# A plan with other durations, and the first half of the first group ahead of everything: a four-stage transformer block on one core

## The chip, the core and the metric

The kernel runs on one core of one Trainium2 chip. The metric is the device time of one execution in microseconds (us). A core has five engines that work side by side, each through its own list of instructions in order: TensorE (PE, matrix products), VectorE (DVE), ScalarE (ACT), GpSimd (POOL) and SyncE (SP, which here issues every DMA). An instruction that waits for another engine holds up everything behind it on its own engine.

## The reference

`x` is 8 sequences of 1024 rows of 256 numbers, all in fp32. Four stages follow each other; each is added to its own input:

```python
x = x + attn_0(layernorm(x))   # linear "flow" attention, 16 heads of 16, then a GELU feed-forward of 1024
x = x + ffn_0(layernorm(x))    # ReLU feed-forward, 256 -> 1024 -> 256
x = x + attn_1(layernorm(x))   # one head of softmax attention, 256 wide, over 1024 rows
x = x + ffn_1(layernorm(x))    # weights and activations rounded to blocks of FP4, SiLU gate, 256 -> 704 -> 256
```

The change touches mostly the first stage. Its core, for each head (`cumsum` runs over the rows of a sequence):

```python
q, k = sigmoid(q), sigmoid(k)
sink_in  = normal / sum_d((q + EPS) * (cumsum(k) + EPS))      # normal = 1, 2, 3, ...
src_out  = normal / sum_d((k + EPS) * (cumsum(q) + EPS))
cons_sink = sum_d((q + EPS) * (cumsum(k * src_out) + EPS)) / normal
cons_src  = sum_d((k + EPS) * (cumsum(q * sink_in) + EPS)) / normal
sink_alloc = sigmoid(cons_sink)
src = exp(clip(cons_src, -1, 1))
v = v * src / cumsum(src) * normal
x = ((q * sink_in / normal) @ cumsum(k^T v)) * sink_alloc
```

`cumsum(k^T v)` makes this causal: within a chunk of 128 rows the kernel forms the scores `k q`, keeps those with key not after query, and multiplies by `v`; what earlier chunks contribute comes from a running sum of `k^T v` (the tile `kv_sum`). The scores are sums of products of sigmoids, so they are positive.

## The kernel before, in words

Rows are worked on in **chunks** of 128 and **groups** of four chunks (512 rows); there are 16 groups, two to a sequence. For the first stage:

- `front` normalises a chunk (`n`) and transposes it into `n0T`; it also adds a bias to the chunk on GpSimd (`res`).
- `linear_span` takes a group, or in group 0 a half group of two chunks ("near"): projections to `q` and `k` (sigmoid on ACT), running sums (`running`, a scan on DVE with a carried column, `carry_cur` or `carry_w`), products with the other of `q` and `k` (`prod`), sums over the 16 numbers of a head as PE products with `hsum`, a reciprocal, and the weights `flow`, which are spread again over the rows of a head: by DMA through DRAM (`packed`, `spread`) for a whole group, by a PE product with a mask (`spread_near`) for a half group. Then the same again with weighted tiles, and from those sums `e`, `div` and `scale`.
- `linear_chunk` scales `v`, makes the zero-padded queries `qz`, four banks of scores, masks them (`sc`, by a product with `triu` on DVE), multiplies with `v` (`sc,v_pad`), adds the running `kv_sum`, projects with `wo`, adds `res`, normalises (`h`), and transposes into a `half` of two chunks.

`dense` runs both feed-forward layers by half groups: for each of eight slices of 128 hidden columns, two products `half,w_ff`, an activation on ACT (`hidden`), and two products `w_ff,hidden` a few slices later. `norms_1` and `norms_2` are the layer norms after them. `soft_chunk` does the third and fourth stage of one chunk, once its whole sequence has been normalised.

**What sets the order.** All this is written as Python generators, "parts", that yield what the next step needs: an engine (`pe`, `dve`, `act`, `dma`), tiles, free PSUM banks, a buffer, a due time `at`. `Plan.run` picks, at each step, the part that has to wait least for PE, then the one whose operands have been ready for long enough (`RIPE`), then the one with the earliest due time. `Plan.took` gives each recorded instruction a duration by a formula for its engine, and keeps when each engine and each tile is free. All five engines are pinned to this order of issue (`add_manual_dep` in `Queue`), so it is the plan's durations, not the chip's, that decide the order in which each engine works. A wrong duration makes no wrong result; it makes an engine wait in front of an instruction whose operands aren't there yet. The due times are in units of groups: `p + 0.1`, `p + 0.15` and so on for group `p`; the second half group of group 0 is due 0.25 later (`after`).

Every instruction is issued by one helper, so all have the same line, L315, in the profile; the tiles' names tell them apart. On PE there are two "tiled" forms (`prod,hsum`, `sc,v_pad`, `q,kv_sum`, `v_pad,k` on 32 columns and `qz,k` on 32 rows), of which four run side by side. An fp32 product is recorded as two passes, a transpose as one.

Of the kernel before, what the change touches and what calls it, by code (L numbers as in the profile page):

```python
# [16 lines left out]
P = 128  # L17
# [12 lines left out]
G = 4  # L30
# [32 lines left out]
class Plan:  # L63
# [12 lines left out]
    def __init__(self, tc, nc):  # L76
# [14 lines left out]
        self.act_set = 0  # L91
        self.tiled = False
# [65 lines left out]
    def took(self, queue, op, args, kw):  # L158
# [11 lines left out]
        after = 0.06  # L170
        if queue == "tensor":
# [3 lines left out]
            cost = size * (0.84e-3 if op == "transpose" else 1.68e-3)  # L175
            tiled = op == "matmul" and (kw["lhsT"].shape[-1] <= 32 or kw["lhsT"].shape[0] <= 32)
            if tiled:
                cost *= 0.25
# [4 lines left out]
        elif queue == "vector":  # L183
            each = {"reciprocal": 6.2e-3, "tensor_tensor_scan": 2.15e-3}.get(op, 1.05e-3)
            cost = 0.15 + each * size
            if op == "tensor_scalar" and outs[0].dtype == BF16:
                cost = 0.16 + 0.26e-3 * size
        elif queue == "scalar":
            cost = (0.16 if op == "copy" else 0.26) + 0.82e-3 * size
            for x in args:  # L190
                if not isinstance(x, bass.AP) and self.SETS.get(x, self.act_set) != self.act_set:
                    self.act_set = self.SETS[x]
                    cost += 1.3
# [8 lines left out]
        start = self.free.get(queue, 0.0)  # L202
        for ap in aps:
            name = ap.tensor.name
            if self.by.get(name) != queue:
                start = max(start, self.done.get(name, 0.0))
            if name not in self.done and name in self.held:
                start = max(start, self.used[name])
        if queue == "tensor":
# [4 lines left out]
            self.ran = start + cost  # L214
        end = start + cost
# [6 lines left out]
        self.free[queue] = end  # L222
# [30 lines left out]

    def ready(self, need):
# [19 lines left out]
    def run(self):  # L274
        while self.parts:
            now = self.free.get("tensor", 0.0)
            best = None
            for part in self.parts:
# [5 lines left out]
                wait = max(max(t) - now - (0.3 if stays else 0.0), 0.0)  # L284
                unripe = max(t[1] + self.RIPE[queue] - now, 0.0)
# [48 lines left out]
def block_stack_kernel(ctx: ExitStack, tc: tile.TileContext, a: dict, out: bass.AP):  # L334
# [115 lines left out]
    pos = const.tile([P, P], F32, name="pos")  # L450
    nc.vector.tensor_copy(pos, pos_i)
# [20 lines left out]
    mask_tiles = [make("prob", "mask") for _ in range(2)]  # L472
    late = set()

    def masks():
        yield act(ident, at=0.02)
        for b in range(4):
# [12 lines left out]
    def late_constants():  # L490
# [10 lines left out]
        late.add("hsum")  # L501
        yield dve()
# [3 lines left out]
        for g in range(NG):  # L506
            yield dve()
            nc.vector.tensor_scalar(rpos[:, g, :], pos, float(g * GT), None, ALU.add)
            yield dve()
            nc.vector.reciprocal(rpos[:, g, :], rpos[:, g, :])  # L510
# [71 lines left out]
    def layernorm_affine(dst, src, gain, shift):  # L582

        mean, rstd = ln_stats(src)
# [7 lines left out]
    def turned(srcs):  # L592
# [4 lines left out]
        return bank[:, : len(srcs), :]  # L597

# [213 lines left out]
    def running(out, cur, carry, b, first, last):  # L812
# [9 lines left out]
        if not last:  # L822
            nc.vector.tensor_copy(carry[:, b : b + 1], out[:, cur.shape[1] - 1 :])
# [45 lines left out]
    def linear_group(p):  # L869
# [34 lines left out]
        for i in range(G):  # L904
            plan.start(front(i), p + 0.03 * i)
# [19 lines left out]
    def linear_span(p, span, fronts, tiles):  # L925
# [13 lines left out]
        after = 0.25 if span.start else 0.0  # L939
        near = len(span) < G  # L940

# [32 lines left out]
        for n, b in enumerate((2, 0, 3, 1)):  # L974
            other = (b + 2) % 4
            prods[other] = yield from fresh(
                "flow", dve(cur[b], at=p + 0.15 + 0.04 * n + after, when=turn("flow")), "prod"
            )
            prod = prods[other][:, :width]
            running(prod, cur[b], past["cur"], b, opens, closes)  # L980
            yield dve(cur[other])
            nc.vector.scalar_tensor_tensor(prod, cur[other], ATT_EPS, prod, ALU.add, ALU.mult)
# [6 lines left out]
        nc.vector.scalar_tensor_tensor(flow, pos[rows], float(g * GT), r1, ALU.add, ALU.mult)  # L989
# [7 lines left out]
        for n, b in enumerate((2, 0, 3, 1)):  # L997
            other = (b + 2) % 4
            w = weighted[b]
            need = dve(w, at=p + 0.35 + 0.04 * n + after, when=turn("scale"))  # L1000
            if near:
                weighted[b] = yield from fresh("flow", need, "weighted")
            else:
                yield need
            out = weighted[b][:, :width]
            nc.vector.tensor_tensor(out, cur[b], w[:, :width], ALU.mult)
            if near and n % 2:
                plan.let_go(w)
            prods[other] = yield from fresh("flow", dve(), "prod")
            prod = prods[other][:, :width]  # L1010
            running(prod, out, past["w"], b, opens, closes)
            plan.drop(weighted[b])
            yield dve()
            nc.vector.scalar_tensor_tensor(prod, cur[other], ATT_EPS, prod, ALU.add, ALU.mult)
# [34 lines left out]
        nc.vector.scalar_tensor_tensor(e, pos[rows], float(g * GT), e, ALU.add, ALU.mult)  # L1049
        nc.vector.tensor_scalar(e, e, src[rows], None, ALU.mult)  # L1050
# [34 lines left out]
    def linear_chunk(p, i, n0T, comp, qk):  # L1085

        s, g = divmod(p, NG)
        past, c = seqs[s]["past"], p * G + i
        here = slice(i * P, (i + 1) * P)
# [6 lines left out]
        for k in range(2):  # L1096
# [25 lines left out]
                at=p + 0.62 + 0.06 * i,  # L1122
# [7 lines left out]
        qz = tile_qz.rearrange("p (k e t) -> p k e t", k=2, e=2)  # L1130
        for e in range(2):
# [4 lines left out]
        yield pe(qz, banks=4, tiled=True)  # L1136
        banks = []
        for r in range(4):
            rows = slice(32 * r, 32 * r + 32)
            bank = mm_bank()  # L1140
            banks.append(bank)
            for k in range(2):
# [4 lines left out]
                    start=True,  # L1147
                    stop=True,
                )
        plan.drop(tile_qz)  # L1150
        scores = []
        for bank in banks:
            sc = yield from fresh("flow", dve(bank), "sc")
            sc = sc.rearrange("p (n t) -> p n t", n=4)
# [473 lines left out]
```

## Time and profile before

| | us |
|---|---|
| median of three runs | 2684.94 (2684.01 to 2687.68) |
| the profiled execution, its own time | 2683.53 |
| span of its instructions | 2681.8 |
| granted PE clock, mean | 0.991 of full |
| PE idle before `hsum` products, waiting for `prod`, whole span | 12.3, in 11 waits |
| PE idle waiting for `n` | 11.2, in 7 waits |
| PE idle waiting for ACT `prob` | 7.7, in 9 waits |
| ACT table loads | 320 of 1283 ns |
| DVE masking of scores, 128x512 | 256 of 681 ns |

In a row of the profile, `bank<-half,w_ff` is a product that reads `half` and `w_ff` and writes a PSUM bank, `x4` are four records in a row, and `[4.28 <-DVE prod]` says that the engine stood idle for 4.28 us before it and that the instruction of DVE that writes `prod` ended the wait. PEclk is the clock that the chip granted PE.

### The profile page before, as it was taken

The page shows a single profiled execution, that of the slowest core. Times are in us where ns is not written, and L with a number is a line of the kernel's source. Part 1 is how long each engine was busy: PE and PEld are TensorE (multiplying, and loading weights), DVE is VectorE, ACT ScalarE, POOL GpSimd, SP SyncE. Part 2 cuts the span into 40 slices and gives each one's busy share as a digit, 9 for nine tenths or more (in the row PEclk, how much of TensorE's full clock was granted, in tenths as well). Part 3 has the DMA queues.
Part 4 walks back from the last instruction along what each step waited for, and adds up shares of the span by engine and source line. Part 5 has one row for each costly group of instructions (what it writes and reads, how often), then busy time and mean ns, then how long its engine had stood idle before and what let it go on. Part 6 is the DMA issues. An engine that isn't in the chain of part 4 may idle for free.

```text
span 2681.8 us, 45726 instructions
## 1 busy us (share of the span) xinstructions
PE 2600.9 (97%) x16687; PEld 2016.8 (75%) x16687; DVE 1971.2 (74%) x4514; ACT 1258.6 (47%) x2442; POOL 585.4 (22%) x1101
## 2 busy tenths in 40 slices
PE   6999999999999999999999999999999999999998
PEld 4777777787777777777777777777777777787765
DVE  8779787867768768586786858778586876856576
ACT  2443544445444453545536464363544546344343
POOL 1332322222212313123131212213122131212000
PEclk8999999999999999999999999999999999999999
DMA  3334231323223222232323223132231322322100
GB/s 87 101 106 144 85 101 58 107 66 87 73 64 107 75 77 72 77 101 62 97 66 94 81 72 107 52 90 79 68 108 58 97 64 73 91 66 82 41 12 12
DMA packets 286815, 211.89 MB, mean 79 GB/s; under 512 B 24704, under 2 KB 275072, under 8 KB 286592
## 3 DMA queue, kind: packets, MB, share of 16 engines
q1 hardware_dynamic: 286592, 208.97, 26.7%
q8 instruction: 133, 2.18, 0.3%
q14 instruction: 90, 0.74, 0.1%
HBM read 188.17 MB, written 20.71 MB: 78 GB/s over the span
## 4 chain that ended last, share of the span: by engine, by line
PE 72%; DVE 18%; DMA 4%; ACT 2%; issue 1%; POOL 1%; SPq 0%; DVEq 0%; ACTq 0%; POOLq 0%
PE bank L315 72%; DVE prod L315 3%; DVE hid L315 2%; DMA spread<-packed 2%; DVE n L315 2%; DVE ln_st L315 1%; DVE div L315 1%; DVE u L315 1%; DVE spread L315 1%; DVE x_amax L315 1%; DVE res L315 1%; ACT L315 1%; DVE e L315 1%; DVE mx L315 1%; DVE q L315 1%
## 5 line engine op out<-in xcount | busy, mean ns | idle before, releaser
L315 PE MATMUL bank<-half,w_ff 128*128 128x256 f32 x2048 | 532.5, 383 | 8.3 <-DMA w_ff<-in_L_ffn_w_dram 3.8
L315 PE MATMUL bank<-w_ff,hidden 128*128 128x256 f32 x2048 | 530.5, 383 | 0.0
L315 ACT ACT_TABLE_LOAD x320 | 410.6, 1283 | 81.2 <-PE bank L315 76.6
L315 PEld LDWEIGHTS bank<-half,w_ff 128*128 128x128 f32 x2048 | 380.2, 191 | 81.7 <-issue 23.9
L315 PEld LDWEIGHTS bank<-w_ff,hidden 128*128 128x128 f32 x2048 | 370.1, 191 | 83.9 <-issue 39.3
L315 POOL TENSOR_SCALAR ln_ve<-ln_mv 128x1 f32<-128x1 f32 x384 | 95.5, 249 | 1434.3 <-DVE ln_mv L315 1424.2
L315 ACT ACTIVATE hidden<-bank,c_L_ffn_b 128x256 f32<-128x256 f32 x256 | 121.0, 473 | 319.0 <-PE bank L315 318.8
L315 POOL TENSOR_TENSOR ln_rstd<-ln_ve,neghalf 128x1 f32<-128x1 f32 x384 | 240.8, 627 | 32.0
L315 PE MATMUL bank<-n2T,qT 128*128 128x512 f32 x512 | 241.6, 595 | 0.9 <-ACT qT L315 0.9
L315 PE MATMUL bank<-vt,probT 128*128 128x256 f32 x1024 | 233.5, 382 | 0.0
L315 PEld LDWEIGHTS bank<-vt,probT 128*128 128x128 f32 x1024 | 194.3, 191 | 29.9 <-issue 2.3
L315 ACT ACTIVATE hidden<-bank,c_L_attn_b 128x256 f32<-128x256 f32 x256 | 121.6, 475 | 171.0 <-PE bank L315 169.5
L315 PE MATMUL bank<-wdT,hqT 128*128 128x256 f32 x768 | 178.4, 383 | 1.9 <-ACT hqT L315 1.9
L315 PE MATMUL bank<-wgT,xqT 128*128 128x352 f32 x512 | 173.6, 462 | 1.1 <-ACT xqT L315 0.9
L315 PE MATMUL bank<-wuT,xqT 128*128 128x352 f32 x512 | 172.4, 459 | 0.0
L315 DVE TENSOR_TENSOR sc<-bank,triu 128x512 f32<-128x512 f32 x256 | 159.8, 681 | 13.8 <-PE bank L315 13.4
L315 PEld LDWEIGHTS bank<-wdT,hqT 128*128 128x128 f32 x768 | 145.4, 192 | 22.5 <-ACT hqT L315 2.8
L315 DVE TENSOR_TENSOR hid<-hid,bank 128x352 f32<-128x352 f32 x118 | 60.9, 516 | 131.5 <-PE bank L315 88.2
L315 PEld LDWEIGHTS bank<-n2T,qT 128*128 128x128 f32 x512 | 93.1, 190 | 72.1 <-issue 63.3
L315 PEld LDWEIGHTS bank<-wuT,xqT 128*128 128x128 f32 x512 | 97.4, 190 | 54.1
L315 PEld LDWEIGHTS bank<-wgT,xqT 128*128 128x128 f32 x512 | 93.4, 190 | 39.5 <-issue 6.0
L315 DVE TENSOR_REDUCE mx<-bank 128x1 f32<-128x512 f32 x128 | 86.7, 677 | 45.7 <-PE bank L315 45.2
(214 smaller groups left out, 4365.0 us busy)
## 6 DMA issues: line engine op xcount, KB each, us to landing
w_ff<-in_L_attn_W_dram SPq DMA_DIRECT2D x512, 128.0 KB
w_ff<-in_L_ffn_w_dram SPq DMA_DIRECT2D x512, 128.0 KB
spread<-packed SPq DMA_DIRECT2D x90, 256.0 KB
x<-in_L_attn_inputs_dram SPq DMA_DIRECT2D x64, 128.0 KB
xr<-in_L_attn_inputs_dram SPq DMA_DIRECT2D x64, 128.0 KB
rows<-res SPq DMA_DIRECT2D x64, 128.0 KB
out_dram<-y SPq DMA_DIRECT2D x64, 128.0 KB
rows<-rows SPq DMA_DIRECT2D x56, 128.0 KB
```

The costliest lines, as they stand in the source:

```text
L315: ins = method(*args, **kw)
```

## The change

It has these parts; the order of the instructions changes on every engine from the first ten microseconds to the end.

- `Plan.took`: other durations. A result is ready for other engines 0.035 instead of 0.06 after its end; DVE and ACT instructions overlap by 0.08 and 0.1; PE columns cost 0.853e-3 and 1.687e-3 instead of 0.84e-3 and 1.68e-3; bf16 products cost a quarter; a table load is charged to the engine and not to the result; reading an accumulator costs 0.15; outputs wait for their last readers; DVE and GpSimd wait also for their own results; a DMA waits for the eighth DMA before it to land.
- GpSimd steps get a `yield` of their own (`plan.pool`), so that the plan places them when their operands are there; in `norms_1` the addition to `xr`, which waits for a DMA, now stands behind the statistics.
- The carried columns are copied by ACT instead of DVE, with a `yield`; the flows go in pairs (scan, scan, product, product). A product overwrites the tile that the copy reads.
- `kv` of both halves is multiplied by `bdiag` in one DVE instruction; `pos` has a slice for each of the two groups of a sequence; `e` takes one instruction fewer.
- `table`: ahead of `hidden`, where the function set changes, a one-column activation that needs no product, so that the table load stands ahead of the wait for the bank.
- Group 0's first two chunks are due one unit earlier (`at`, negative), and a part with negative due time is taken 0.3 earlier and needs not be ripe; the second half group's `after` of 0.25 stays.
- In group 0 (`by_act`) the mask is a bf16 product: `later` holds an identity and, for each position that has to go, -2^100; it is multiplied into the bank first, the scores are added, and ACT takes the Relu into `sc`. For the other groups DVE masks as before.

```diff
@@ Plan.took
-        after = 0.06
+        overlap, after = 0.0, 0.035
         if queue == "tensor":
...
-            if tiled:
+            if tiled or op == "matmul" and kw["lhsT"].dtype == BF16:
                 cost *= 0.25
...
+            overlap = 0.08
         elif queue == "scalar":
...
-                    cost += 1.3
+                    self.free[queue] = self.free.get(queue, 0.0) + 1.3
+            if kw.get("accum_out") is not None:
+                cost += 0.15
+            overlap = 0.1
...
+        if queue not in ("tensor", "sync"):
+            start = max([start] + [self.used.get(ap.tensor.name, 0.0) for ap in outs])
         for ap in aps:
             name = ap.tensor.name
-            if self.by.get(name) != queue:
-                start = max(start, self.done.get(name, 0.0))
+            if self.by.get(name) != queue or queue in ("vector", "gpsimd"):
+                start = max(start, self.done.get(name, 0.0) + (0.05 if queue == "gpsimd" else 0.0))
...
+        if queue == "sync":
+            start = max(start, self.landed.pop(0))
...
-        self.free[queue] = end
+        self.free[queue] = end - overlap
@@ Plan.run
-                wait = max(max(t) - now - (0.3 if stays else 0.0), 0.0)
-                unripe = max(t[1] + self.RIPE[queue] - now, 0.0)
+                wait = max(max(t) - now - (0.3 if stays or part[2] < 0.0 else 0.0), 0.0)
+                urgent = part[2] < 0.0
+                unripe = 0.0 if urgent else max(t[1] + self.RIPE[queue] - now, 0.0)
@@ late_constants
+        yield dve(triu)
+        nc.vector.tensor_scalar(
+            later[:, :GT].rearrange("p (n t) -> p n t", n=4),
+            triu.unsqueeze(1).to_broadcast([P, 4, P]),
+            -1.0,
+            2.0**100,
+            ALU.add,
+            ALU.mult,
+        )
@@ table, new
+    def table(func):
+        if plan.act_set != plan.SETS.get(func, plan.act_set):
+            nc.scalar.activation(small([P, 1], "table", 1), one, func)
@@ running
-            nc.vector.tensor_copy(carry[:, b : b + 1], out[:, cur.shape[1] - 1 :])
+            yield act(out)
+            nc.scalar.copy(carry[:, b : b + 1], out[:, cur.shape[1] - 1 :])
@@ linear_group
-            plan.start(front(i), p + 0.03 * i)
+            plan.start(front(i), p + 0.03 * i - (p == 0 and i < 2))
@@ linear_span
-        after = 0.25 if span.start else 0.0
+        after = 0.25 if span.start else -1.0 if near else 0.0
...
-        for n, b in enumerate((2, 0, 3, 1)):
...
+        for n, pair in enumerate(((2, 0), (3, 1))):
+            for b in pair:
+                need = dve(cur[b], at=p + 0.15 + 0.08 * n + after, when=turn("flow"))
+                prod = prods[(b + 2) % 4] = (yield from fresh("flow", need, "prod"))[:, :width]
+                yield from running(prod, cur[b], past["cur"], b, opens, closes)
+            for b in pair:
+                yield dve(cur[b], prods[b])
+                nc.vector.scalar_tensor_tensor(
+                    prods[b], cur[b], ATT_EPS, prods[b], ALU.add, ALU.mult
+                )
@@ linear_chunk
+        by_act = p == 0
...
+        banks = [mm_bank() for _ in range(4)]
+        for bank in banks:
+            if by_act:
+                nc.tensor.matmul(
+                    bank, lhsT=later[:, GT:], rhs=later[:, :GT], start=True, stop=False,
+                    skip_group_check=True,
+                )
...
-            sc = yield from fresh("flow", dve(bank), "sc")
+            sc = yield from fresh("flow", (act if by_act else dve)(bank), "sc")
             sc = sc.rearrange("p (n t) -> p n t", n=4)
+            if by_act:
+                nc.scalar.activation(sc, bank.rearrange("p (n t) -> p n t", n=4), AF.Relu)
+                scores.append(sc)
+                continue
...
+            yield plan.pool(new)
...
+        yield plan.pool(h)
         nc.gpsimd.tensor_tensor(rc, h, b2, ALU.add)
@@ norms_1
-        nc.gpsimd.tensor_tensor(xr, xr, ln2b, ALU.add)
...
-        yield from layernorm_affine(xc, u, ln2g, xr)
+        stats = ln_stats(u)
+        yield plan.pool(xr)
+        nc.gpsimd.tensor_tensor(xr, xr, ln2b, ALU.add)
+        yield from layernorm_affine(xc, u, ln2g, xr, stats)
```

## The prediction

> **What bounds the kernel now.** I read four views in this order: the page, the windows by stage, the waits of the matmul engine (PE) by stage, and the timeline of the first 75 us. The page first:
>
> ```profile
> span 2681.8 us, 45726 instructions
> PE 2600.9 (97%) x16687; PEld 2016.8 (75%) x16687; DVE 1971.2 (74%) x4514; ACT 1258.6 (47%) x2442; POOL 585.4 (22%) x1101
> PE   6999999999999999999999999999999999999998
> PEclk8999999999999999999999999999999999999999
> ```
>
> PE bounds it; DVE, the next engine, has a quarter of the span free. A plan that only orders the same work can win no more than the time in which PE stands still or runs slowly. The windows show where that is:
>
> ```profile
> 0.00:91.00 91.00, 67.51 (x557) 50.31 (x558) 73.22 (x194) 28.28 (x68) 23.26 (x56) 0.81 0.30 78
> 91.00:300.00 209.00, 194.46 (x1513) 156.26 (x1512) 174.56 (x435) 85.63 (x208) 61.60 (x119) 0.98 0.42 122
> 300.00:2500.00 2200.00, 2173.88 (x13910) 1690.77 (x13909) 1602.61 (x3611) 1073.94 (x2027) 492.35 (x905) 1.00 0.27 80
> 2500.00:2682.00 182.00, 165.05 (x713) 119.46 (x711) 120.79 (x276) 70.80 (x140) 8.23 (x22) 0.98 0.05 15
> ```
>
> The columns are stretch, length, busy time of PE, weight load, DVE, ACT and POOL, then clock and DMA. PE idles 91 - 67.5 = 23.5 us of the first 91 and has 0.81 of its clock there, which is 0.19 x 91 = 17 us more; it idles 14.5 us from 91 to 300, 26 in the 2200 us after that, 17 in the tail. So some 98 us are to be had at all, 40 of them in the first 3% of the span. Who is waited for in those first 91 us:
>
> ```profile
> PE bank L315 <- DVE prod L315: 8.5, 7, 4.3
> PE bank L315 <- DVE n L315: 7.8, 2, 7.4
> PE bank L315 <- DVE scale L315: 2.6, 1, 2.6
> ```
>
> And from 300 to 2500 (us in total, times, longest):
>
> ```profile
> PE bank L315 <- DVE v L315: 6.5, 9, 1.1
> PE bank L315 <- ACT prob L315: 5.4, 7, 1.4
> PE bank L315 <- DVE n L315: 3.4, 5, 1.1
> ```
>
> There all waits are short and come to 26 us. The timeline of the start:
>
> ```profile
> 29.36 0.42 DVE L315 SCALAR_TENSOR_TENSOR prod<-q,prod 128x256 f32<-128x256 f32 x1
> 29.70 0.74 DVE L315 TENSOR_TENSOR_SCAN prod<-one,carry_cur,q 128x256 f32<-128x256 f32 x1
> 29.84 1.07 PE L315 MATMUL bank<-prod,hsum 128*32 128x128 f32 x8 [4.28 <-DVE prod L315]
> 35.41 0.28 DVE L315 TENSOR_TENSOR e<-bank,rpos 64x128 f32<-64x128 f32 x1
> 40.18 0.28 DVE L315 TENSOR_TENSOR scale<-e,div 64x128 f32<-64x128 f32 x1
> 50.29 3.67 DVE L315 TENSOR_TENSOR sc<-bank,triu 128x512 f32<-128x512 f32 x6
> 65.27 0.25 PE L315 MATMUL bank<-ident,scale 64*128 64x64 f32 x1 [2.64 <-DVE scale L315]
> 73.92 1.97 PE L315 MATMUL bank<-half,w_ff 128*128 128x256 f32 x4
> ```
>
> The scan with carry_cur belongs to the second half group and stands in front of the first half group's last products. The two are interleaved, each waits for the other's DVE work, and PE's first feed-forward product comes at 73.92. A 0.42 us DVE instruction is followed by one that doesn't need it after 0.34 us: 0.08 us of overlap, which the old plan does not count (it charges 0.42 and adds 0.06).
>
> **What the Trainium skill says.** "TensorE: Matmul & The Clock Gate", Part 1 (the HAM clock gate), gives half clock after an idle window of about 3.4 us. The trace agrees: PE idles 4.28 us up to 29.84, and its clock is 0.50 from 30 to 40 and 0.58 from 40 to 50 us. The same page, Back-to-back issue gap, prices a bf16 product of 512 columns at N/2.4 + 2.5 = 216 ns; no run before has one. "VectorE: DVE Perf Modes", The DRAIN you can't avoid, lets the next operation start when the pipe is empty; the trace shows the 0.08 us of overlap above, so the measurement decides. "ScalarE: Activation LUTs", What ACT_TABLE_LOAD costs, has 1283 ns a load; the trace has 1283 on 320 of them.
>
> **The change part by part.** Orders are read from the two built programs, durations from the rows of before.
>
> 1. The first half group goes first. Up to the first scan DVE's list is nearly the same: one more constant (about 0.6 us, nearest row a 128x512 operation at 0.68), two additions of 0.21 moved earlier. But scans no longer stand behind the normalisation of chunks 2 and 3 (two n, 12.76 to 14.47): first scan at about 12.7 instead of 14.39. Four scans (0.69), four products (0.35) and the two n (0.4) are 5.0 us, so 17.7; the product now overwrites what ACT's carry copy reads, and that copy stands behind the fourth sigmoid (done at about 15.7), which I price at 1.0: 18.7 against 19.69. Reciprocal, flow and the mask product took 3.5 us to the first weighting (23.20); I take 3.1, since one projection fewer is ahead on PE: 21.8. Then before needs 12.2 us to e (35.41). After: 4 x (0.45 + 0.70) + 4 x 0.37 = 6.1, plus two scans and one product of the second half, 1.9: e at 29.8. From e to the end of scale 5.05 us, less one 0.28 operation, plus some of the second half: 34.7 against 40.46. To the scaling of q 4.9 us before, as the second half's mask product and a v product were ahead; now the transpose and one 2.07 us product, 2.5: 37.2 against 45.39. qz is done 2.5 us later, 39.7.
>
> 2. Causal mask by product and ACT, in group 0 only. DVE loses 16 operations of 0.68, ACT gains 16 of about the same (prob, also 128x512 out of PSUM, has 0.684, start to start about 0.6), PE gains 16 bf16 products: 16 x 0.216 = 3.5 us. Bounds: 1 us if most fall into waits, 14 us if they go like fp32 (0.86 each). I take 3.5; the built program has them as one pass with a weight load each. ACT needs 7 x 0.6 and a copy before the first output product: 39.8 + 4.6 = 44.4 against 52.97. That product to the second chunk's output projection took 8.6 us; with the kv multiplication in one instruction and no scores on DVE I take 6.6, so 51, and 6 us more for that product, the layer norm with the second half's operations in between, the transposes and the copy: first feed-forward product at about 57 against 73.92.
>
> 3. What PE gains from it. The second half's scale does not come earlier: after 34.7 DVE has 23.6 us of operations ahead of its end by the rows of before, and some 7 of waits (q 2.5, kv 3.5, pool 1), which gives 65.3, give or take 1.5 (65.11 before). By then the new order has on PE, ahead of that scale's transpose, 5 half,w_ff and 2 w_ff,hidden pairs, one wqk_T pair (8 x 0.87), six small items (1.4): 8.3 us that before does later. From there before runs at half clock until 75 us and loses another 4 us; after, PE has been busy since 57. Less the masks: 8.3 + 4 - 3.5 = 9, and 1 for the earlier chunks 2 and 3: **-10** (bounds -15 and -4).
>
> 4. Durations of the plan. DVE cheaper by its overlap, PE dearer by 1.5%, accumulate reads at 0.15, pool 0.05 later, DMA issue limited by landings. They order everything after 91 us. From 91 to 300 PE waits 4.4 us for w_raw, 3.1 for w_ff, 2.5 for qz, 2.0 for scale, which are orders in which the plan thought something ready that was not; I let half go: **-6** (bounds -12 and +6). From 300 on 26 us: the reads after prob, 0.197 each, were not in the plan at all and prob costs 5.4. A plan without the excess on DVE also has less slack. I take **-5** (bounds -15 and +20).
>
> 5. PE switches between tiled and untiled 246 instead of 264 times by the built orders; at 0.1 to 0.25 us each, from starts in the timeline, 18 x 0.15: **-2**.
>
> 6. Moved GpSimd steps, carry copies on ACT (72 of 0.154), kv in one operation (56 fewer), table loads 321 to 290 with a 0.2 us operation ahead that takes them out of the wait for the product: they relieve DVE by some 30 us and POOL from waits behind xr, but neither bounds. At no cost they are hidden by PE at 99% from 300 to 2500. If that cover goes, the carry copies cost first: each makes the product wait for ACT, about 0.4 us, behind whatever ACT waits for.
>
> 7. Tail: the last four chunks stand as before in PE's order: 0 (bounds +-4).
>
> Sum: -10 - 6 - 5 - 2 = -23. Against the profiled execution's own 2683.53 that is 2660.5; the median of the runs is 1.4 above it, so 2662.
>
> **Rivals.** A: only the start. Plan durations move waits without reducing them: for it speaks that they are 1.2% of 300 to 2500 already; -10 - 2 + a few = 2675. B, slower: the plan's slack was what kept PE fed. DVE and ACT are charged less, so consumers are placed on PE nearer to their operands, and the new carry copies add a crossing from DVE to ACT and back that stands behind ACT's waits (ACT hidden waits 0.5 to 5 us for PE again and again). Waits of 26 us from 300 on would have to rise beyond 26 + 18 = 44 to pay the other terms back; doubled and with the 91 to 300 part at its bad end, -12 + 30 + 6 = +24, 2708. Against it: the old prices differ from the trace's (0.42 where 0.34 passes, no accumulate read), the new ones are close to it. C: the half group's chain gains all it can and the early and steady waits mostly go: -15 - 12 - 13 - 2 = -42, 2643. That the first half is not really in front is unlikely: the built order shows it.
>
> **How the numbers follow.** My forecast (2652 to 2671) has 0.55, A (2671 to 2681) 0.17, C 0.11, B 0.17. A measurement here tells 0.2%, 5.4 us, from no change; that takes 0.03 of A and 0.04 of B: faster 0.80, same 0.07, slower 0.13. The range leaves out the far ends of B and C: 2642 to 2684.
>
> **What would show it.** First feed-forward product near 57 us and e near 30: step 1 and 2; second scale still near 65: step 3; a clock under 0.7 from 57 on, or PE waiting over 3 us for that scale, would take most of the 10 back. The bf16 products at 0.2 us start to start. Waits of PE under 10 us from 91 to 300, near 20 from 300 to 2500. Wrong if those last grow past 40, above all on prod or u behind ACT copies.

## The result, and the profile after

| | before | after |
|---|---|---|
| median of the runs, us | 2683.88 (2678.24 to 2687.68, 20 runs) | 2688.58 (2684.87 to 2693.58, 20 runs) |
| after / before | | 1.0021 [1.0015, 1.0028] |
| the profiled execution, its own time, us | 2683.53 | 2685.22 |
| span of its instructions, us | 2681.8 | 2683.5 |

The changed kernel is slower by 0.2%, where 2662 us was forecast. From the page of the kernel after:

```profile
span 2683.5 us, 45556 instructions
PE 2595.0 (97%) x16702; PEld 2017.4 (75%) x16703; DVE 1930.8 (72%) x4353; ACT 1248.2 (47%) x2604; POOL 589.9 (22%) x1101
PE   6898999999999999999999999999999999999997
PEclk8999999999999999999999999999999999999999
L332 ACT ACT_TABLE_LOAD x289 | 370.8, 1283 | 5.1
```

Every engine does about what the diff says: DVE has 40 us less, table loads fall from 320 to 289. None of it shows in the time: PE is busy for 97% of the span, as before. The windows, in the columns used for the kernel before:

```profile
0.00:91.00 91.00, 65.95 (x544) 49.99 (x546) 67.68 (x178) 44.36 (x118) 21.73 (x54) 0.91 0.32 87
91.00:300.00 209.00, 189.43 (x1515) 149.72 (x1514) 168.83 (x392) 84.38 (x206) 66.06 (x119) 0.97 0.40 115
300.00:2500.00 2200.00, 2180.45 (x13970) 1703.60 (x13968) 1579.99 (x3524) 1053.92 (x2147) 494.70 (x909) 1.00 0.28 81
2500.00:2684.00 184.00, 159.15 (x678) 114.13 (x677) 114.29 (x261) 65.54 (x134) 7.43 (x20) 0.95 0.05 15
```

PE's clock in the first 91 us is 0.91 instead of 0.81, as hoped. Its idle time there didn't fall: 25.1 us, 23.5 before. And PE now idles 19.6 us from 91 to 300 (14.5 before) and 25 in the tail (17). Only the long middle has less idle time, 19.6 instead of 26.1. Whom PE waits for from 91 to 300:

```profile
PE bank L332 <- DMA w_ff<-in_L_ffn_w_dram: 5.2, 2, 4.2
PE bank L332 <- ACT qz L332: 4.2, 2, 4.0
PE bank L332 <- DVE q_c L332: 3.2, 1, 3.2
PE bank L332 <- DVE n L332: 3.0, 3, 2.1
```

And from 2500 on:

```profile
PE bank L332 <- DVE q L332: 7.3, 1, 7.3
PE bank L332 <- DVE hid L332: 6.0, 3, 4.3
```

Idle time leaves out slow clocks and small gaps, and equal times don't hold equal work. So I also count **excess**: time less what PE's instructions up to that point need at the rate of the trace, 216 ns start to start for 256 fp32 columns or 512 bf16 ones, in proportion for other widths, a quarter for the tiled forms. Stretches are cut at 75, 300 and 2400 us of PE's own work:

| us | PE's work | excess to 75 | 75 to 300 | 300 to 2400 | to the end | span |
|---|---|---|---|---|---|---|
| before | 2488.6 | 54.7 | 31.0 | 88.0 | 19.5 | 2681.8 |
| after | 2491.8 | 47.8 | 40.3 | 76.1 | 27.5 | 2683.5 |

So the start wins 6.9 us and pays 3.2 for the mask products; 9.3 are lost right after it; 11.9 are won in the middle; 8 are lost at the end. Each figure is from one execution. In e9 below, whose order is the changed kernel's up to its last 60 us, the first three stretches come out within 0.3, 2.3 and 1.6 us of the changed kernel's, so differences of that size tell nothing. The experiments ask which of the losses and gains belong to the change.

### The profile page after: what moved, and what is told of

It is laid out like the page before. It is cut to its first block, busy times and chain, and to the rows that moved or that the text cites. A ratio compares the mean times of both kernels' runs of the same rounds, so it can differ in the third digit from the quotient of the medians.

```text
span 2683.5 us, 45556 instructions
## 1 busy us (share of the span) xinstructions
PE 2595.0 (97%) x16702; PEld 2017.4 (75%) x16703; DVE 1930.8 (72%) x4353; ACT 1248.2 (47%) x2604; POOL 589.9 (22%) x1101
## 4 chain that ended last, share of the span: by engine, by line
PE 85%; DVE 9%; DMA 2%; ACT 2%; POOL 1%; issue 1%; SPq 0%; DVEq 0%; ACTq 0%; POOLq 0%
PE bank L332 85%; DMA spread<-packed 1%; DVE prod L332 1%; DVE n L332 1%; DVE hid L332 1%; DMA packed<-scale 1%; DVE ln_st L332 1%; DVE q L332 1%; ACT L332 1%; DVE x_amax L332 0%; DVE u L332 0%; DVE res L332 0%; SPq L332 0%; POOL ln_rstd L332 0%; DVE w_raw L332 0%
## 5 line engine op out<-in xcount | busy, mean ns | idle before, releaser
L332 POOL TENSOR_SCALAR ln_ve<-ln_mv 128x1 f32<-128x1 f32 x384 | 107.0, 279 | 1753.3 <-DVE ln_mv L332 1740.0
L332 PEld LDWEIGHTS bank<-w_ff,hidden 128*128 128x128 f32 x2048 | 370.8, 191 | 87.3 <-issue 38.7
L332 DVE TENSOR_TENSOR sc<-bank,triu 128x512 f32<-128x512 f32 x240 | 150.7, 679 | 10.9 <-PE bank L332 9.9
L332 PE MATMUL bank<-ident,n 128*128 128x128 f32 x512 | 94.3, 278 | 25.2 <-DVE n L332 13.9
```

The source lines that it names most:

```text
L332: ins = method(*args, **kw)
```

## The experiments

### The parts alone: e1, e2, e3

e1 is the changed kernel without the early start and without the mask products; e2 has the early start but masks on DVE; e3 is the kernel before plus the early start and the mask products, with the old durations.

```diff
@@ e1 (e2: only the last line, and no mask products)
-            plan.start(front(i), p + 0.03 * i - (p == 0 and i < 2))
+            plan.start(front(i), p + 0.03 * i)
-        after = 0.25 if span.start else -1.0 if near else 0.0
+        after = 0.25 if span.start else 0.0
-        at = p - (p == 0 and i < 2)
+        at = p
-        by_act = p == 0
+        by_act = False
```

> The change without its start: due times of the first half group and the mask as before, all durations and other edits kept. Theory 1 (each part has its own sign; the new durations cost about 9 us from 75 to 600 us and give 14 from there to 2400): 2680 to 2686, no stall pattern of the start of the change, first feed-forward product back near 74 us. Theory 2 (the order is chance: any new durations reshuffle the waits before 600 us and in the tail): anything from 2674 to 2694. If the start was the whole loss: below 2679.

> The change with group 0 masked on DVE as before, first half group still in front. Theory 1: PE saves 16 x 0.216 = 3.5 us, DVE gets 16 x 0.68 back, half of it in the chain of the first half group: first feed-forward product 2 to 4 us later than 60, in all 0 to -4 against the change, 2684 to 2689. Theory 2: within 6 us of the change either way, and the difference arises after 91 us.

> The kernel before with only the first half group in front and the mask product of group 0; old durations, carries on DVE. Theory 1: the start's own gain, some 5 us at 75 us, survives: 2677 to 2681. Theory 2: the gain at 75 us is there, but the end is anywhere within 6 us of before.

Measured against the kernel before: e1 2686.17 us, 1.0003 [0.9994, 1.0011]; e2 2691.21, 1.0017 [1.0010, 1.0023]; e3 2690.13, 1.0027 [1.0021, 1.0034]. The early start brings the first feed-forward product to 56 to 60 us in e2 and e3, and neither is faster for it. Masks on DVE with the early start (e2) leave 63.3 us of excess up to 75, against 47.8 with the products: there the products are worth 15.5 for 3.2. By 300 only about 2.4 of that is left (93.7 without them, 88.1 + 3.2 with them). The tail keeps a lone wait of 7.3 us on `q` in e1 and e2, which share the durations and the moved steps with the changed kernel.

### How far an order moves by itself: e4, e5, e11, e12

The plan's price of a PE column is moved by about 0.1%. Nothing is added or removed; only ties and near ties fall differently.

```diff
@@ e4 (e11: 0.852e-3, 1.685e-3)
-            cost = size * (0.853e-3 if op == "transpose" else 1.687e-3)
+            cost = size * (0.854e-3 if op == "transpose" else 1.689e-3)
@@ e5, on the kernel before (e12: 0.839e-3, 1.678e-3)
-            cost = size * (0.84e-3 if op == "transpose" else 1.68e-3)
+            cost = size * (0.841e-3 if op == "transpose" else 1.682e-3)
```

> The change with PE 0.1% dearer in the plan (0.854e-3 and 1.689e-3): no content. Theory 1: within 0.1% of the change, 2686 to 2691. Theory 2: the order differs and the time moves by 3 to 8 us, by waits in other places before 600 us and in the tail.

> The kernel before with one thing changed: the plan's price of a PE column is 0.12% higher (0.841e-3 and 1.682e-3). No instruction is added or removed. Theory 1 (the change's own contents and prices cost the time): this has none of them, so within 0.1% of the kernel before, 2682 to 2687 us. Theory 2 (the order of the kernel before was a lucky draw, above all its tail, where the last two chunks stand side by side on PE; in this build the last chunk stands alone as in the changed kernel): slower by 4 to 14 us, with PE waiting 4 to 8 us once for the last chunk's q and a tail (from the last w_ff,hidden to the end) near 181 us instead of 173.9.

> The changed kernel with the plan's price of a PE column 0.12% lower (0.852e-3, 1.685e-3); nothing added or removed. If the order is a draw: anywhere in 2678 to 2700 us, most likely 2 us or more away from the changed kernel's 2688.6, with the same tail (7.3 us wait on q) and the difference in the excess from 500 to 2250 us of PE's work, which has been 80 to 98 us over ten orders. If the prices matter in a smooth way, the nudge upward having cost 12 us: about 12 us less, 2676 to 2680, or (a price at its best) up to 12 more.

> The kernel before with the plan's price of a PE column 0.12% lower (0.839e-3, 1.678e-3); nothing added or removed. If the order is a draw: 2676 to 2696 us. If the price acts in a smooth way, the nudge upward having won 7 us: about 7 us slower than before, 2689 to 2692. If the old prices as such make a better order than the changed kernel's: below 2686, as both old-price kernels without the new start so far (2683.8 and 2676.6).

Measured: e4 2700.67 us, 1.0054 [1.0042, 1.0067]; e5 2676.59, 0.9974 [0.9966, 0.9982]; e11 2699.68, 1.0055 [1.0043, 1.0068]; e12 2664.29, 0.9921 [0.9907, 0.9936]. A nudge with no content moves the time by 7 to 20 us. From here on I call such a result a **draw**: it depends on how near ties happen to fall in the plan. My second theory had the scale right and, for e5, the sign wrong: the kernel before was not a lucky draw. e12 fell 12 us below the range that I had given to a draw. The price doesn't act smoothly either, as both nudges of the changed kernel cost 11 to 12 us by the medians (9 by the ratios). The windows from 600 to 2300 us, PE alone (stretch, length, busy time, clock, DMA), of the kernel before:

```profile
600.00:2300.00 1700.00, 1680.55 (x10780) 1.00 0.28 80
```

of the kernel after:

```profile
600.00:2300.00 1700.00, 1689.72 (x10841) 1.00 0.28 82
```

of e4:

```profile
600.00:2300.00 1700.00, 1681.59 (x10767) 1.00 0.28 81
```

and of e12:

```profile
600.00:2300.00 1700.00, 1696.89 (x10888) 1.00 0.28 82
```

The 9 us that the changed kernel wins there are gone in e4, with the same durations; e12 has only 3 us of idle time in 1700 us with the old ones. So the middle is a draw. It isn't noise of the measurement, since e9 repeats the changed kernel's excess from 300 to 2400 (77.7 and 76.1).

### Carry copies and the latency of a DMA: e6, e8

```diff
@@ e6
-            yield act(out)
-            nc.scalar.copy(carry[:, b : b + 1], out[:, cur.shape[1] - 1 :])
+            yield dve(out)
+            nc.vector.tensor_copy(carry[:, b : b + 1], out[:, cur.shape[1] - 1 :])
@@ e8
-            after = self.free["rings"] - end + 1.8
+            after = self.free["rings"] - end + 3.0
```

> The changed kernel with the carried columns copied by DVE again, so that no product of DVE stands behind a copy of ACT. If the crossing from DVE to ACT and back is what costs in the changed kernel (the mechanism of rival B): faster by 3 us or more, and PE's waits on prod and u fall. If it is hidden, as step 6 of the prediction has it: the same waits on prod within 2 us, and the time moves only as far as any other order does (the nudge of the changed kernel moved it by 12 us); the tail stays near 182 us with a 7 us wait on q.

> The changed kernel with the plan's latency of a DMA at 3.0 instead of 1.8 us; nothing else. Of PE's waits from 91 to 300 us some 11 us are for a w_ff that stood on SP behind a spread waiting for its DRAM round trip, for qz and q_c that wait for the scale's spread, and for n behind a spread on DVE. Theory 1 (the plan thinks DMAs early and puts their readers too near): these fall by 5 us or more, idle time from 91 to 300 near 14 us instead of 19.6, and the time falls by 3 to 8 us, to about 2682. Theory 2 (such waits come from SP's own order, not from the latency, and every other order draws anew): idle time from 91 to 300 stays within 3 us of 19.6 and the whole lies anywhere from 2683 to 2700.

Measured: e6 2686.83 us, 1.0011 [1.0002, 1.0020]; e8 2686.41, 1.0010 [1.0004, 1.0017]. In e6 PE's waits on `prod` in the first 91 us fall from 5.3 to 2.2 and 4.5 come up on `carry_cur`: the crossing to ACT costs nothing that can be told from a draw. In e8 the idle time from 91 to 300 falls by 2.1 us to 17.4, less than the 5 expected, but the excess from 75 to 300 falls from 40.3 to 31.0; e6 has 32.4 there without touching the latency. So these waits can be avoided with the early start, but neither run shows that a wrong latency makes them. What both won there went in the middle (82.1 and 83.7 instead of 76.1).

### The tail: e9, e10, e17

Only the due time of the last chunks of the third and fourth stage (`soft_chunk`) is changed: in e9 on the changed kernel, in e10 on e5, in e17 on e12.

```diff
@@ e9, e10 (e17: min(cc, 61)), in soft_chunk and where it is started
-        at = 3 + cc / 4
+        at = 3 + (cc - 2 * (cc == 63)) / 4
```

> The changed kernel with the last chunk of all due half a unit earlier, so that the last two chunks stand side by side on PE as in the kernel before. The order is the changed kernel's up to the last 25 groups of products, some 60 us before the end; no instruction is added or removed. If the lone last chunk is what the tail costs: the 7.3 us wait for q falls to 0 to 2, the tail goes from 182 to 175 to 178 us, and the time falls by 4 to 7 us, to 2681 to 2684. If the tail is bounded by DVE's rounding to FP4 whatever the order: the wait only moves to hid or n, and the time stays within 2 us of the changed kernel's.

> The nudged kernel before (2676.59 us, PE price 0.12% up) with the last chunk of all due half a unit earlier, so that the last chunks go side by side to the end. Its tail has a lone wait of 4.5 us on the last chunk's q. If lone chunks at the end cost as in the changed kernel (7.3 us gone, 8.9 us of time won): that wait falls under 2 us and the time by 3 to 6 us, to 2671 to 2674. If the wait only moves to hid or n of the chunks before, as 3.7 us of the changed kernel's did: 2675 to 2678.

> The best order so far (the kernel before with the PE price 0.12% down, 2664.3 us) with the last two chunks due together with the one before them, so that three stand side by side at the end. The order is e12's up to the last sixth of the tail. If the tail's cost is one chunk's FP4 rounding with nothing beside it: e12 waits 2.6 us once on hid there and 1.8 on flow; 2 to 6 us less, 2658 to 2662. If the tail of e12 is already free of it: 2662 to 2666.

Measured: e9 2679.68 us, 0.9986 [0.9977, 0.9995]; e10 2671.73, 0.9943 [0.9930, 0.9957]; e17 2661.01, 0.9906 [0.9892, 0.9920]. The timeline of PE at the end (start, length), first after:

```profile
2656.71 1.11 PE L332 MATMUL bank<-ident,hid 128*128 128x128 f32 x4 [4.29 <-DVE hid L332]
...
2666.23 1.35 PE L332 MATMUL bank<-wuT,xqT 128*128 128x352 f32 x4
2674.85 1.51 PE L332 MATMUL bank<-ident,q 128*128 128x128 f32 x6 [7.28 <-DVE q L332]
```

then e9:

```profile
2657.88 1.35 PE L332 MATMUL bank<-wuT,xqT 128*128 128x352 f32 x4
2659.07 2.75 PE L332 MATMUL bank<-wdT,hqT 128*128 128x256 f32 x12
2665.50 1.54 PE L332 MATMUL bank<-ident,hid 128*128 128x128 f32 x6 [3.68 <-DVE hid L332]
...
2672.21 0.82 PE L332 MATMUL bank<-ident,q 128*128 128x128 f32 x6
```

In the changed kernel the last chunk's gate and up products end at 2667.6, and PE then has nothing until DVE has rounded that chunk (`q`) to FP4: 7.28 us. In e9 they stand beside the chunk before, two roundings overlap, and the wait for `q` is gone. The excess to the end falls from 27.5 to 19.5, the kernel before's value. With one due time the changed kernel is faster than the kernel before. e10 and e17 win 6.8 and 3.1 us of such excess (20.8 to 14.0, 17.8 to 14.7). In e17 a wait of 2.5 us for `q` comes up while those for `hid` fall from 5.1 to 2.2. e17 is the fastest kernel of the study.

### The early start in six pairs: e13, e14, e15, e16

e13 and e16 are e3 with the prices of e5 and e12; e14 and e15 are e1 with those of e4 and e11. Each has a partner that differs in the early start and mask products alone.

```diff
@@ e14 (e15: 0.852e-3, 1.685e-3), on e1
-            cost = size * (0.853e-3 if op == "transpose" else 1.687e-3)
+            cost = size * (0.854e-3 if op == "transpose" else 1.689e-3)
@@ e13 (e16: 0.839e-3, 1.678e-3), on e3
-            cost = size * (0.84e-3 if op == "transpose" else 1.68e-3)
+            cost = size * (0.841e-3 if op == "transpose" else 1.682e-3)
```

> The start of the change alone (first half group in front, mask by a product and ScalarE) on the nudged old plan: to be set against the nudged kernel before, 2676.59 us, as the start alone on the old plan (2690.13) was against the kernel before (2683.8 to 2684.8, so +5 to +6). If the start itself costs time, by what it does to the stretch from 75 to 300 us: again slower by 4 to 8 us, 2681 to 2685. If its own worth is the gain of 5 us that stands at 75 us and the rest is the draw of the order: it lies 5 us below the nudged kernel before on average, within a scatter of 8, so 2664 to 2680. In both the first feed-forward product stands near 56 us instead of 74.

> The new durations and steps without the start (as e1), PE price 0.12% up; its pair with the start is e4, 2700.7 us. If the start costs net time: below 2696, near e1's 2686. If the new prices nudged up make a bad order whatever the start: within 5 us of 2700. The tail again near 182 us, with 7 us on the last chunk's q or k.

> The new durations and steps without the start (as e1), PE price 0.12% down; its pair with the start is e11, 2699.7 us. If the start costs net time: below 2695. If the start's own worth of 5 us stands and the rest is a draw: anywhere from 2684 to 2706. The tail again near 182 us.

> The start alone on the old durations, PE price 0.12% down; its pair without the start is e12, 2664.3 us. If the start costs net time on the old durations: 2675 to 2695 (its two pairs so far: +6 and +17). If e12 was a lucky draw and the start is worth its 5 us: the mean of the draws, 2675, less 5, so 2660 to 2680. PE's excess time at 75 us of its work is then again near 57 us plus 3 us of masks, no less than without the start, as in e3 and e13.

Measured, median in us and ratio to the kernel before; the intervals of the four new ones are e13 [1.0016, 1.0040], e14 [0.9993, 1.0009], e15 [1.0024, 1.0049], e16 [0.9928, 0.9953]:

| durations, nudge | without the start | with the start | difference of ratios |
|---|---|---|---|
| old, none | before, 1 | e3 2690.13, 1.0027 | +0.0027 |
| old, up | e5 2676.59, 0.9974 | e13 2693.54, 1.0028 | +0.0054 |
| old, down | e12 2664.29, 0.9921 | e16 2669.29, 0.9941 | +0.0020 |
| new, none | e1 2686.17, 1.0003 | after 2688.58, 1.0021 | +0.0018 |
| new, up | e14 2685.48, 1.0001 | e4 2700.67, 1.0054 | +0.0053 |
| new, down | e15 2693.95, 1.0036 | e11 2699.68, 1.0055 | +0.0019 |

All six have the same sign: the early start with its masks costs 5 to 14 us, 8.5 on average. In two pairs (e12 and e16, e15 and e11) the intervals overlap, and every pair also sets one draw against another; it is the common sign that carries the claim. The masks are not the whole of it: e2, the start without mask products, is 0.0014 above e1, and the masks' own work is 3.4 us. e13 is slower than both of its theories allowed. The new durations, read down the table, give -0.0006 to +0.0115, +0.0047 or 12.5 us in the mean: never a clear gain, and rather a loss, though most of it comes from the pairs in the last row. The stretches, each the mean of three profiled orders, show where:

| us | PE's work | excess to 75 | 75 to 300 | 300 to 2400 | to the end |
|---|---|---|---|---|---|
| old | 2488.6 | 55.0 | 31.0 | 80.1 | 19.4 |
| old, start | 2492.0 | 55.1 | 32.5 | 81.4 | 23.0 |
| new | 2488.6 | 58.6 | 28.5 | 84.6 | 26.5 |
| new, start | 2491.9 | 49.0 | 38.8 | 87.3 | 27.6 |

With the new durations the start wins 9.6 us by its first 75 us of work, pays 3.3 for the masks and gives 10.3 back by 300: 36.9 to 40.3 in the three orders with it, 27.2 to 29.6 in the three without. e8 and e6, which have the start too, have 31.0 and 32.4 there, so a loss remains but its size is not fixed. With the old durations the start wins nothing by 75 us, and its cost is the masks (3.4) and 1.3 to 3.6 us in each later stretch. The middle lies between 68.8 and 93.2 in all twelve.

One date moves the same way in all six pairs, that of the second half group's `scale` on DVE. With the start it comes 4.0, 6.3 and 5.2 us later than without it on the new durations, and 21.1, 21.5 and 13.7 us later on the old ones. Group 1's `scale` is later on PE in all six as well, by 1 to 4 us (new) and 11 to 20 us (old).

### Who gives the start back: e18, e19

Three dates tell it, from PE's timeline: the first, 65th and 129th record of `half,w_ff` (group 0's first and second feed-forward layer, group 1's first) are at 74, 125, 182 us before, and at 60, 122, 183 after. A lead of 14 us is 3 at the second layer and none at group 1. DVE is late here, in the timeline of the kernel after:

```profile
70.20 0.29 DVE L332 TENSOR_TENSOR scale<-e,div 64x128 f32<-64x128 f32 x1
```

This is the second half group's scale; it starts at 64.83 in the kernel before. Preparing the FP4 and softmax weights is allowed from the first feed-forward product on (`count["stage"] == 4`), so it too came earlier. e18 holds it back until the second half group is scaled; e19 does the same on e16, with e17's tail.

```diff
@@ e18
-                        dma(at=1.5 + 1.6 * i / len(pieces), when=lambda: count["stage"] == 4),
+                        dma(at=1.5 + 1.6 * i / len(pieces), when=lambda: 2 in groups[0]["scaled"]),
-            raw = two((yield from fresh("prob", dma(at=1.3, when=lambda: count["stage"] == 4), "wqk_raw")))
+            raw = two((yield from fresh("prob", dma(at=1.3, when=lambda: 2 in groups[0]["scaled"]), "wqk_raw")))
```

> The changed kernel, in which the loads of the FP4 and softmax weights wait until the second half group is scaled, instead of the first feed-forward product. In this build no weight rounding stands ahead of the second half group's scale on DVE. If weight preparation pulled forward is what gives the gain of the start back: that scale ends on DVE at 65 to 67 us instead of 70.5, group 1's scale reaches PE at 142 to 145 us instead of 149, and the excess of PE's work from 75 to 300 falls from 42 to 31 to 35 us; the whole lies near 2680, give or take 8 for the later order. If group 1's chains are limited anyway: the scale comes earlier, but the excess from 75 to 300 stays at 38 or more, or what it loses is added up to 75.

> The start on the old durations, PE price 0.12% down (e16, 2669.3 us), with the weights' loads held back as in e18 and the last two chunks due with the one before them as in e17. If both repairs add up: 10 us for the start's stretch and 3 for the tail, 2653 to 2660, less than any kernel so far (2661.0). If the order after 300 us is drawn anew: within 12 us of 2666.

Measured: e18 2682.88 us, 1.0001 [0.9992, 1.0009]; e19 2665.10, 0.9941 [0.9929, 0.9954]. DVE in e18, with nothing of the weights in between:

```profile
60.60 0.42 DVE L332 SCALAR_TENSOR_TENSOR prod<-q,prod 128x256 f32<-128x256 f32 x1
63.75 0.29 DVE L332 TENSOR_TENSOR e<-bank,rpos 64x128 f32<-64x128 f32 x1 [2.73 <-PE bank L332]
64.09 0.35 DVE L332 TENSOR_SCALAR e<-e,upper,lower 64x128 f32<-64x128 f32 x1
67.42 0.48 DVE L332 TENSOR_TENSOR_SCAN div<-src,ahead,e 64x128 f32<-64x128 f32 x1 [2.98 <-ACT ahead L332]
...
69.81 0.29 DVE L332 TENSOR_TENSOR scale<-e,div 64x128 f32<-64x128 f32 x1
```

and PE in e18:

```profile
59.92 2.08 PE L332 MATMUL bank<-half,w_ff 128*128 128x256 f32 x4 [0.46 <-ACT half L332]
61.93 1.77 PE L332 MATMUL bank<-prod,hsum 128*32 128x128 f32 x16
63.63 1.99 PE L332 MATMUL bank<-half,w_ff 128*128 128x256 f32 x8
65.47 0.28 PE L332 MATMUL bank<-total,front 128*128 128x1 f32 x2
```

The scale comes only 0.4 us earlier, so the weights were not what held it; that part of my expectation failed. What holds it begins much earlier, with `r`, the reciprocal from which the chain's first weights `flow` come. Before:

```profile
36.23 0.96 DVE L315 RECIPROCAL r<-bank 64x128 f32<-64x128 f32 x1 [0.17 <-PE bank L315]
```

In the kernel after, on DVE and on PE:

```profile
45.47 0.96 DVE L332 RECIPROCAL r<-bank 64x128 f32<-64x128 f32 x1 [3.48 <-PE bank L332]
42.29 1.04 PE L332 MATMUL bank<-later 128*128 128x512 bf16 x4
43.26 1.17 PE L332 MATMUL bank<-qz,k 32*128 32x256 f32 x16
44.35 1.07 PE L332 MATMUL bank<-prod,hsum 128*32 128x128 f32 x16
```

The first half group's chain now stands ahead of the second half's, and the head sums for `r` stand on PE behind the first half's masks and scores. So `r` comes 9.2 us late. (On the old durations `r` is 22 to 25 us later with the start than without.) The chain then catches up. Its last `prod` ends at 61.17, 58.04 before, so 3.1 of the 5.4 us of delay are there before a feed-forward product is in the way.

The feed-forward work adds most of the rest. From that `prod` to `e` DVE took 1.4 us before and takes 3.0 now. In e18, as the lines above show, the last `prod` ends at 61.02, but PE starts the head sums at 61.93, after four `half,w_ff` at half speed, and DVE has their bank at 63.75; the small product `total,front`, which `ahead` needs, stands behind eight more. Then ACT, in the kernel after:

```profile
65.20 0.18 ACT L332 ACTIVATION_READ_ACCUMULATOR e<-e,sign 64x1 f32 x1
65.40 1.28 ACT L332 ACT_TABLE_LOAD   x1
66.70 0.20 ACT L332 ACTIVATE table<-one 128x1 f32<-128x1 f32 x1
66.81 0.46 ACT L332 ACTIVATE hidden<-bank,c_L_attn_b 128x256 f32<-128x256 f32 x1
67.16 0.36 ACT L332 COPY wqk_T<-bank 128x256 f32<-128x256 f32 x1
67.55 0.15 ACT L332 COPY ahead<-bank 64x1 f32<-64x1 f32 x1
```

The table load that the change puts ahead of `hidden` stands in front of `ahead`, the link of the chain: `total,front` ends at 66.39 in this kernel, and ACT copies its result at 67.55. From `e` to the scan that reads `ahead` it is 3.6 us, 2.3 before; from there to `scale` 0.6 are won back, with one instruction fewer. In all, from the first half group's scale to the second's DVE was idle for 4.2 us before (24.7 less 20.5 busy), after for 12.5 (35.7 less 23.2): 3.5 of them for `r`, 1.7 for `e`, the others mostly in steps of the first half group.

Something is won later in e18 all the same: group 1's scale is on PE at 145.0 instead of 148.9, the excess up to 300 is 80.8 instead of 88.1, and e18 is level with the kernel before. With the mask products counted it is 3.8 us ahead of e1 at 300 (80.8 + 3.3 against 87.9), where the changed kernel is 3.4 behind (88.1 + 3.2). Of the 7.3 us half came from 75 to 300 and half ahead of it, so my 31 to 35 for that stretch was missed by 1.6 (36.6). That the weights brought forward are part of what the start gives back is not shown by this one order: e8 and e6 come to 80.9 and 82.3 up to 300 with the weights as early as in the changed kernel. e19 is 4.2 us below e16, with 6.3 less excess up to 300 and 5.4 less at the end, but 6.6 more in the middle; it is 4.1 us above e17, which has no early start. The two repairs did not add up, and of its two expectations the second holds, a new draw after 300 us.

## Why the prediction was wrong, step by step

1. **The first half group first.** Right. DVE ran the first scan at 12.18 (12.7 forecast), `e` at 30.37 (29.8), `scale` ended at 34.83 (34.7).
2. **Mask products.** Right: the trace has 15 of them, and within a run of three or four they start 215 to 226 ns apart, 216 in most cases, the price of "TensorE: Matmul & The Clock Gate", Back-to-back issue gap. The first feed-forward product came at 60.06 (57 forecast), after a wait of 4.49 us on the second `h`:

```profile
58.94 0.66 PE L332 MATMUL bank<-ident,h 128*128 128x128 f32 x2 [4.49 <-DVE h L332]
60.06 2.07 PE L332 MATMUL bank<-half,w_ff 128*128 128x256 f32 x4 [0.46 <-ACT half L332]
```

   The same page's Part 1 gives half clock after such an idle window; the four products took 2.07 us, and 1.03 a few us later, which agrees. PE's clock was 0.50 from 57.0 to 63.7 us: the sign that I had named against the 10 us came true.
3. **-10 from the start: failed.** Two terms. "The second half's scale does not come earlier" was taken as unchanged, 65.3; it was on DVE 5.4 us later than before, and later in all six pairs. I had priced 23.6 us of DVE operations (23.2 measured, 3.9 of them weight preparation) and 7 us of waits; the idle time was 12.5, because the work moved ahead (the first half's scores, then feed-forward products, a table load and `hidden`) stands in the chain's way on PE and ACT. And I counted work moved ahead of that scale as time won. By 75 us of PE's work 6.9 less 3.2 for the masks were won, 3.7 instead of the 9 of the sum, and what was won is clock: PE's idle time up to 91 us rose by 1.6. Work moved ahead is kept only if what follows can start earlier too, and group 1, whose chains follow the second half's, did not: 10.3 us more from 75 to 300 in the mean of three orders with the new durations. The start as a whole costs 8.5 us on average. Which wait takes how much of the 10.3 stays open.
4. **-6 from 91 to 300, -5 from 300 on: failed.** The first was +5.1 of idle time. Without the start, the new durations change the excess from 75 to 300 by -2.5 in the mean, so the rise appears only together with the start; it isn't forced by it, as e6 and e8 have 17.6 and 17.4 us of idle time there instead of 19.6. The second came out at -6.6 of idle time and looks right, but two nudges of the same plan take it away (26.2 in e4, 30.9 in e11): it was a draw, and the waits that new prices should have removed (`prob`, `v`) are there in both.
5. **Mode switches, -2.** Not tried by itself.
6. **Moved steps, 0.** The carry copies: nothing that can be told (e6). The table load ahead of its wait delays a chain's link that is queued behind it on ACT, as the lines above show; what that costs by itself was not tried.
7. **Tail, 0 (bounds -4 and +4): failed, +8.** I compared the last four chunks in PE's order and overlooked that the last one's gate and up products had moved behind the down product of the one before. All six orders with new durations have 22.9 to 30.3 us there, means 26.5 and 27.6; the old ones 17.8 to 26.7, means 19.4 and 23.0. e9 shows the mechanism, and e10 and e17 that it holds in other orders. Which of the new prices makes the plan end so stays open.

Rival B had the sign, not the mechanism: PE's waits from 300 to 2500 fell. They rose in one draw (30.9 us in e11), but e6 found no cost in the copies by ACT. What no case held was how far any order is from its neighbour: the twelve orders span 36 us, more than the sum forecast.

## What to carry to other kernels

Where a plan's prices set an order, nudge a price that means nothing before you believe a difference: here 0.12% moved the time by up to 20 us, so one order against one order tells little below 1%, and several nudges a side show what is systematic. Work moved to the front is won only if the stage that follows can start earlier too; so look for the date of the next stage, and for the queues in which the moved work now stands ahead of that stage's chain. At the end of a kernel leave no chunk alone whose vector work nothing covers.

## What was unexpected of the hardware

Nothing of the single operations: durations were those of the kernel before. Unexpected was how much room there was at the same work: e17 does the same products as the kernel before (2488.6 us of PE's work in both) in a span of 2659.3 us instead of 2681.8, by order alone.
